# Four edits at the stage boundaries of a convolution and attention kernel: who writes a place-holding tile, when the next image's norm is computed, when the feed-forward begins, and who gathers the last image's rest

## The chip, the cores and the metric

The kernel runs on one core of a Trainium2 chip. The metric is the device time in microseconds of one execution. Times given for the whole kernel are medians of several executions; durations of single instructions come from one profiled execution. TensorE is called PE, VectorE DVE, ScalarE ACT, GpSimd POOL and SyncE SP, as in the profile.

## The reference

The input is four images of 128 channels by 64x64 points (4096 tokens), float32. Each image goes through a non-local layer whose scores compare all tokens with all tokens; the whole then goes through an attention layer with its feed-forward, and through a linear layer with a batch norm and a scan. Of the reference, shortened:

```python
# layer 0, on the group-normalised image
y = einsum('oc,nchw->nohw', w, x) + b; e1, e2, asm = prelu(y)   # w1/w2 (64 rows), wa (128 rows)
score = softmax(einsum('nci,ncj->nij', e1, e2), axis=2)
out = einsum('nij,ncj->nci', score, asm)
# attention over 1024 tokens, 16 heads of size 8, q = k = v
q = qz_ring(heads + rx_theta)              # products of cosines
attn = softmax(q q^T / sqrt(8)); ctx = attn q
x1 = ln(x + ctx @ w_comb.T + b_comb)
zf = cos(x1[..., :8]) * cos(ry_theta)
out = ln(x1 + relu(zf @ w1.T + b1) @ w2.T + b2)
# then Wx = x W, batch norm over all rows, and a scan along the rows with V
```

## The kernel before

The images are worked one after the other, in three stages each; lines are those of the kernel before.

`first_stage` (L1178) is the convolution layer of one image. The image `xs` is normalised to `q` by eight DVE instructions (L331), which need the group statistics: means `gm` and, from POOL's power function (L228), the inverse deviation `r_g`. Then eight pieces give `e1` and `e2`: a matmul (L343), two ACT relus (L294, L295: `ya`/`za` and `yb`/`zb`), one DVE addition (L296); this is the `prelu` of L291. Four pieces give `asmT` (matmuls L351 and L360, then `prelu_vector`: DVE L300 and L301). Then 128 pieces of scoring: a score matmul pair (L384), ACT's exponential (L392), DVE's running sum (L400), and the weighing matmul (L407). After each of these 140 pieces the code calls `meanwhile()`, which issues one step of the image's own next work, and one step of the feed-forward of the image before. `in_steps(waiting, every, most)` hands these out: a new chunk of the feed-forward is begun every `every` calls, at most `most` are open, and every open chunk makes one step per call. There are eight chunks of 27 steps. Of those, DVE's heavier ones are step 2 (the addition `v` L990) and 3 (statistics of `v`), 5 (the normalisation), 7 to 10 (the cosine), 18 (an addition and statistics), 20, 22 and 24 (normalisations and statistics). Step 9 is a sine on ACT, step 17 the matmuls L1042, steps 25 to 27 transposes, the linear layer and its batch norm statistics.

`second_stage` (L1224) is the attention. It works eight pairs of heads, each in four blocks of tokens. PE computes scores (L867), ACT their exponentials (L879), PE the weighing (L720). The score matrix is symmetric: for blocks off the diagonal DVE flips the exponentials (L686) and PE weighs the flipped ones too (L699); these mirror sums are added into `later` (L713). When a block's own sums are complete, `finish` transposes them (`o`, L754) and POOL copies them in 16 pieces into `own` (L762). `mirrored` gathers what the mirror sums give for that block: POOL adds row sums (L736, L741), copies them in 16 pieces (L747), DVE transposes `later` (L777), POOL copies 16 pieces (L787) and adds them (L789, L790). `result` divides (DVE, L794 and L795). For the last pair, three blocks' `mirrored` run at the end of the stage one after the other, each into a `room` of its own, and their three `result` functions are left over: `im["left"]`. The next `first_stage` takes them at its calls 10, 14 and 18.

The next image is prepared in the last block of the last pair: `upcoming` steps through its load (`load_x`, whose issue waits on PE's release of memory) and `norm_stats` (eight statistics L307, their mean L310, and through PE two small products `pg` and `pv`, L312 and L321). `r_g` is computed behind it.

The order of PE, DVE and ACT within these two stages is written by hand (`tc.manual_schedule`): each engine issues its instructions in the order of the code. POOL is ordered by hand in the attention, and by a planner in the convolution. [...] Memory of a stage is laid over the memory of the stage before, and the first writer of a tile waits until the earlier tiles there were read. In `first_stage` one tile, `gap` (6144 floats per partition), holds no data. It stands in the layout so that the tiles behind it come to lie in space that is free early; its first column is written once (L1191), ahead of everything else of the stage.

The last image has no convolution behind it. `third_stage` (L1262) takes its three results and then its feed-forward, eight chunks begun at once, ordered by the planner on all engines. There `fx` is the loaded input of a chunk with a bias added by POOL (L980), `cT` the transposed context (ACT, L983), `v` the sum (L990), `less_v`/L265 its normalisation on ACT with `r_v` from POOL (L228). `hold_every` loads the results of the first three images for the scan (L1287, six loads issued by ACT). The scan follows.

Of the kernel before, what the change touches and what calls it, by code (L numbers as in the profile page):

```python
# [26 lines left out]
def kernel(  # L27
# [31 lines left out]
    nc = tc.nc  # L59
# [264 lines left out]
    def layer0(n, xs, xh, norm, shifted, begin, meanwhile):  # L324
# [23 lines left out]
        for i in range(NIC // 2):  # L348
            pc = pair_psum(f"pa{n}_{i}")
            for j in range(2):  # L350
                nc.tensor.matmul(  # L351
                    pc[:, j, :],
                    ones[ds(32 * j, 1), :],
                    ba_row[ds(32 * j, 1), :].unsqueeze(1).broadcast_to([1, TG, P]),
                    start=True,
                    stop=False,
                    skip_group_check=True,
                )
            for k in range(2 * TG):
                nc.tensor.matmul(  # L360
                    pc[:, k // TG, ts(k % TG, P)],
                    xh[:, ts(2 * TG * i + k, P)],
                    wa_sb,
                    start=False,
                    stop=True,
                    skip_group_check=True,
                )
            to = asmT[:, ts(i, 2 * IC)].rearrange("p (a b) -> p a b", a=2)
            prelu_vector(to, pc, mid_tile(f"za{n}_{i}"), aa_sb)
            meanwhile()  # L370

        if shifted:
# [186 lines left out]
    def attention(n, q, xs, tail, upcoming):  # L559
# [170 lines left out]

            return 2 * NT + (b - NQB // 2) * TG

        def mirrored_sums(pair, b, denom):

            total = small.tile([P, QT, 2], F32, tag="by_key", name=f"by_key{n}_{pair}_{b}")
            nc.gpsimd.tensor_tensor(  # L736
                total, denom[:, ts(b, QT), :], denom[:, ds(NT + b * QT, QT), :], ALU.add
            )
            if b >= NQB // 2:
                odd = total[:, TG:QT, :]  # L740
                nc.gpsimd.tensor_tensor(odd, odd, denom[:, ds(third_sum(b), TG), :], ALU.add)  # L741
            by_token = small.tile([P, QT, 2], F32, tag="by_token", name=f"by_token{n}_{pair}_{b}")
            src = total.rearrange("p (x s) h -> p s x h", s=4)
            dst = by_token.rearrange("p (x a) h -> p a x h", a=4)
            for a in range(4):
                for s in range(4):
                    nc.gpsimd.tensor_copy(dst[ts(s, 32), a], src[ts(a, 32), s])  # L747
            return by_token

        def finish(pair, b, block, later, denom):  # L750


            o = half_tile(f"o{n}_{pair}_{b}")
            nc.vector.transpose(o, block["acc"])  # L754

            tag = f"own{b}" if b < 2 else "own"
            own = once.tile([P, QT, 2, V], F32, tag=tag, name=f"own{n}_{pair}_{b}")
            ov = o.rearrange("p (s a m) -> p s a m", s=4, a=4)
            for h in range(2):
                for x in range(2):  # L760
                    for s in range(4):
                        nc.gpsimd.tensor_copy(  # L762
                            own[ts(s, 32), ts(x, 4), h, :], ov[ts(2 * h + x, 32), s, :, 0:V]
                        )

            def mirrored(room=None):
                while any(g["steps"] and g["block"] <= (pair, met_by[b][-1]) for g in groups):
                    run_flips(TG)
                    run_pending(turn + 2, 16)
                sums = mirrored_sums(pair, b, denom)  # L770


                if room is None:
                    turned = get("turned", f"turned{n}_{pair}_{b}")
                else:
                    turned = room[:, 0 : 2 * P]
                nc.vector.transpose(turned, later[:, ts(b, 2 * P)])  # L777
                tv = turned.rearrange("p (y k a d) -> p k y a d", y=2, k=4, a=4)
                if room is None:
                    other = get("other", f"other{n}_{pair}_{b}")  # L780
                else:
                    other = room[:, ds(2 * P, QT * 2 * D)]
                to = other.rearrange("p (y a h d) -> p h y a d", y=2, a=4, h=2)
                for x in range(2):
                    for h in range(2):
                        for k in range(4):
                            nc.gpsimd.tensor_copy(to[ts(k, 32), h], tv[ts(2 * x + h, 32), k])  # L787
                    at = other.rearrange("p (t h d) -> p t h d", h=2, d=D)
                    nc.gpsimd.tensor_tensor(own[:, :, :, 0:D], own[:, :, :, 0:D], at, ALU.add)  # L789
                nc.gpsimd.tensor_tensor(own[:, :, :, D], own[:, :, :, D], sums, ALU.add)  # L790

            def result():
                inv = small.tile([P, QT, 2], F32, tag="inv", name=f"inv{n}_{pair}_{b}")
                nc.vector.reciprocal(inv, own[:, :, :, D])  # L794
                nc.vector.tensor_tensor(  # L795
                    qb[:, ts(b, QT), ts(pair, 2 * D)].rearrange("p t (h d) -> p t h d", d=D),
                    own[:, :, :, 0:D],
                    inv.unsqueeze(3).broadcast_to([P, QT, 2, D]),
                    ALU.mult,
                )  # L800

            if b == 2:
                ends.append((turn + 8, mirrored))
                ends.append((turn + 12, result))
            elif b > 2:
                late[0:0] = [mirrored, result]
            else:
                late.extend([mirrored, result])
# [40 lines left out]
        for pair in range(NPAIR):  # L849
            keys, queries, qa, later, denom = ready  # L850
            for b in range(NQB):
# [7 lines left out]
                for at, unit in enumerate(tiles):  # L859
# [4 lines left out]
                    for h in range(2):  # L864
                        for x in range(2):
# [5 lines left out]
                                start=True,  # L871
                                stop=True,
                            )
                    es = exps(name, end_of_all and at >= 2)

                    split = off and unit[0] != unit[1]
                    for h in range(2):
# [54 lines left out]
                    if tail and turn > 2 and next(tail, tail) is tail:  # L932
                        tail = None
                        rest()
                    if end_of_all and (at == 2 or at >= QT):
                        next(upcoming, None)
                    fresh = {
                        "in": block,
# [11 lines left out]
                ready = upcoming_pair  # L950
        for it in waiting:
            weigh(it)
        finish(*it["block"])
        while flips or pending:
            next(upcoming, None)
            run_flips(TG)
            run_pending(turn + 2, 16)
        for _ in upcoming:
            pass
        for _, end in ends:  # L960
            end()
        rooms = (None, half_tile(f"room0_{n}"), get("later", f"room1_{n}"))
        for mirrored, room in zip(late[0::2], rooms):
            mirrored(room)
        return late[1::2]

    def feed_forward(im, i, t2_rows, last, final):
# [210 lines left out]
    def first_stage(im, before):  # L1178


        n = im["n"]


        ffn = dict(x1=(HALF, 2), fhalf=(HALF, 6), hT=(MID, 2))
        sums = dict(sums=(MID, 2), half=(HALF, 2), thalf=(HALF, 6))
        rest = dict(e=(BIG, 2), big=(BIG, 1), mid=(MID, 5))
        pools = {**ffn, "gap": ((P, GAP), 1), **rest, **sums}
        psum = dict(ps_acc=(ONE, 1), ps_pair=(MID, 2), ps_one=(ONE, 2), ps_tok=(ONE, 1))
        engines = {nc.tensor.engine, nc.scalar.engine, nc.vector.engine}
        with stage(f"conv{n}", **pools, **psum), tc.manual_schedule(engines=engines):  # L1190
            nc.vector.memset(get("gap", f"gap{n}")[:, 0:1], 0.0)  # L1191
            own, calls = [], [0]
            step_late = in_steps(feed_forwards(before) if before else [], 15, 2)

            def meanwhile(steps=1):

                calls[0] += 1
                if before and calls[0] in (10, 14, 18):
                    before["left"].pop(0)()
                for _ in range(steps):  # L1200
                    step_first(own)
                step_late()

            norm = im["norm"] or list(norm_stats(n, im["xs"]))[-1]
            layer0(
                n,
                im["xs"],
                im["q"],
                norm,
                n == "r",  # L1210
                lambda ic, sums: own.append(tokens(im, ic, sums)),
                meanwhile,
            )
            *own, tail = own
            for g in own:
                for _ in g:
                    pass
            while step_late():
                pass
            while not next(tail):  # L1220
                pass
        return tail
# [39 lines left out]
    def third_stage(im, final):  # L1262

        with stage(
            f"ffn{im['n']}",
            x1=(HALF, NTG),
            fhalf=(HALF, 22),
            hT=(MID, 6),
            ps_one=(ONE, 8),
        ):  # L1270
            for f in im["left"]:
                f()
            step = in_steps(feed_forwards(im, final), 1, NTG)
            while step():
                pass

# [248 lines left out]
```

## Time and profile before

| | |
|---|---|
| median of 3 executions | 7322.82 us (7321.42 to 7324.19) |
| the profiled execution, and its span | 7318.31 us, 7316.6 us |
| mean granted clock of PE | 0.98 |
| PE busy | 6989.7 us, 96% |
| DVE, ACT, POOL busy | 5984.1, 5890.0 and 2772.9 us (82, 81 and 38%) |
| scoring of image 0, first to last (no feed-forward beside it) | 61.56 to 434.8: 373.24 us, PE busy 369.5 |
| scoring of images 1, 2 and 3 (each with a feed-forward) | 469.16, 468.79 and 469.73 us, PE busy 444.3, 443.8 and 444.6 |
| third score pair of images 0 to 3 at | 61.56, 1739.84, 3535.21 and 5320.27 us |
| first `ya` (L294) of images 0 to 2 at | 31.85, 1694.25 and 3500.28 us |
| last `o` (L754) of the last image at | 7037.77 us |

A line of the timeline gives the start of an instruction or a run of equal ones, its length, the engine, the line of the code, the operation, what it writes and reads, and in brackets how long the engine had been idle before it and whose completion ended that. A line of the list of waits gives the engine, its tile and line, then the releasing engine and tile, then the total, the number of waits and the longest. A busy share says nothing of a stage by itself: windows of time have to be compared, and a stage where PE is full is bound by PE even if others are nearly full too.

### The profile page before, as it was taken

The page shows a single profiled execution, that of the slowest core. Times are in us where ns is not written, and L with a number is a line of the kernel's source. Part 1 is how long each engine was busy: PE and PEld are TensorE (multiplying, and loading weights), DVE is VectorE, ACT ScalarE, POOL GpSimd, SP SyncE. Part 2 cuts the span into 40 slices and gives each one's busy share as a digit, 9 for nine tenths or more (in the row PEclk, how much of TensorE's full clock was granted, in tenths as well). Part 3 has the DMA queues.
Part 4 walks back from the last instruction along what each step waited for, and adds up shares of the span by engine and source line. Part 5 has one row for each costly group of instructions (what it writes and reads, how often), then busy time and mean ns, then how long its engine had stood idle before and what let it go on. Part 6 is the DMA issues. An engine that isn't in the chain of part 4 may idle for free. (4 is left out here: it accounts for less than half of the span.)

```text
span 7316.6 us, 225003 instructions
## 1 busy us (share of the span) xinstructions
PE 6989.7 (96%) x93198; PEld 3500.9 (48%) x93198; DVE 5984.1 (82%) x8068; ACT 5890.0 (81%) x11605; POOL 2772.9 (38%) x9929
## 2 busy tenths in 40 slices
PE   8999999998999999999899999999899999999977
PEld 3445555554444555554344455555444455555546
DVE  5678899886778999888677998989777798889964
ACT  3479999994448999998444999999744599999966
POOL 1024444433223454444222354444422344444442
PEclk9999999999999999999999999999999999999988
DMA  1010000000111000000011100000001100000012
GB/s 28 32 35 24 29 20 21 21 20 14 35 40 44 27 21 20 21 24 20 18 32 48 37 21 21 20 27 18 18 26 35 44 32 21 24 29 21 11 59 105
DMA packets 81599, 212.82 MB, mean 29 GB/s; under 512 B 8800, under 2 KB 8832, under 8 KB 79792
## 3 DMA queue, kind: packets, MB, share of 16 engines
q1 hardware_dynamic: 77312, 186.68, 7.5%
q8 instruction: 733, 12.01, 0.7%
q10 hardware_dynamic: 2016, 10.49, 0.4%
q14 instruction: 306, 2.51, 0.1%
q0 software_dynamic: 1232, 1.14, 0.1%
HBM read 141.65 MB, written 56.62 MB: 27 GB/s over the span
## 5 line engine op out<-in xcount | busy, mean ns | idle before, releaser
L879 ACT ACTIVATE e<-s 128x1024 f32<-128x1024 f32 (+1 forms) x3480 | 2946.7, 889 | 59.1 <-PE s L867 35.9
L686 DVE STREAM_TRANSPOSE t<-e 128x1024 f32<-128x1024 f32 x2240 | 2586.3, 1207 | 6.3 <-ACT e L879 3.9
L699 PEld LDWEIGHTS misc<-t,mirror 128*32 128x32 f32 x57344 | 1665.3, 110 | 1403.7 <-issue 1348.6
L699 PE MATMUL misc<-t,mirror 128*32 128x128 f32 x57344 | 1998.7, 274 | 24.9 <-DVE later L713 17.4
L879 ACT ACTIVATE xs<-s 128x1024 f32<-128x1024 f32 (+1 forms) x2152 | 1834.9, 893 | 33.0 <-PE s L867 19.6
L686 DVE STREAM_TRANSPOSE t<-xs 128x1024 f32<-128x1024 f32 x1344 | 1558.2, 1207 | 2.2 <-ACT xs L879 0.8
L720 PE MATMUL acc<-e,q_aug 128*32 128x512 f32 x11360 | 1518.5, 606 | 0.0
L867 PE MATMUL s<-queries,keys 32*128 32x512 f32 x9216 | 1216.9, 494 | 4.1 <-ACT e L879 2.7
L762 POOL COPY own<-o 32x36 f32<-32x36 f32 x2048 | 429.7, 210 | 1750.3 <-DVE o L754 1670.3
L407 PE MATMUL acc<-p,asmT 128*128 128x512 f32 x2048 | 983.3, 612 | 0.0
L392 ACT ACTIVATE p<-s 128x1024 f32<-128x1024 f32 x512 | 497.1, 1022 | 558.5 <-PE s L384 549.6
L720 PE MATMUL acc<-xs,q_aug 128*32 128x512 f32 x7072 | 942.2, 605 | 0.0
L400 DVE TENSOR_TENSOR total<-total,p 128x1024 f32<-128x1024 f32 x448 | 575.2, 1284 | 295.2 <-ACT p L392 271.5
L867 PEld LDWEIGHTS s<-queries,keys 32*128 32x128 f32 x9216 | 479.8, 182 | 490.5 <-issue 367.3
L656 POOL COPY mirror<-q 32x128 f32<-32x128 f32 x2048 | 601.1, 293 | 239.0 <-PE misc L699 151.1
L787 POOL COPY other<-turned 32x64 f32<-32x64 f32 x1920 | 441.1, 230 | 629.4 <-DVE turned L777 550.3
L879 ACT ACTIVATION_READ_ACCUMULATOR e<-s 128x1 f32 x2880 | 649.9, 226 | 0.0
L407 PEld LDWEIGHTS acc<-p,asmT 128*128 128x128 f32 x2048 | 361.5, 192 | 517.2 <-issue 515.0
L384 PE MATMUL s<-e,e 64*128 64x512 f32 x2048 | 520.3, 626 | 5.6 <-DVE asmT L301 5.4
L713 DVE TENSOR_TENSOR later<-later,misc 128x128 f32<-128x128 f32 (+1 forms) x576 | 162.5, 282 | 378.1 <-PE misc L699 373.7
L747 POOL COPY by_token<-by_key 32x4 f32<-32x4 f32 x2048 | 374.5, 183 | 86.4
L720 PEld LDWEIGHTS acc<-e,q_aug 128*32 128x32 f32 x11360 | 225.7, 108 | 347.8 <-issue 330.2
(246 smaller groups left out, 4719.1 us busy)
## 6 DMA issues: line engine op xcount, KB each, us to landing
keys<-parts_dram SPq DMA_DIRECT2D x256, 256.0 KB
queries<-parts_dram SPq DMA_DIRECT2D x1024, 32.0 KB
fx<-x_dram SPq DMA_DIRECT2D x64, 256.0 KB
x_dram<-x SPq DMA_DIRECT2D x56, 256.0 KB
xs<-in_x_dram SPq DMA_DIRECT2D x16, 512.0 KB
t_dram<-t2T SPq DMA_DIRECT2D x32, 256.0 KB
t2s<-t_dram SPq DMA_DIRECT2D x16, 512.0 KB
parts_dram<-high SPq DMA_DIRECT2D x28, 256.0 KB
```

The lines of the kernel that those rows point to most:

```text
L384: nc.tensor.matmul(s[:, j, :], e2[rows, ts(2 * jp + j, P)], e1[rows, ts(ic, IC)], start=True, stop=True,)
L392: nc.scalar.activation(p, s, AF.Exp)
L400: nc.vector.tensor_tensor(state[ic], state[ic], p, ALU.add)
L407: nc.tensor.matmul(state["acc", ic], asmT[:, ts(2 * jp + j, P)], p[:, j, :], start=jp == 0 and j == 0, stop=jp == NP - 1 and j == 1,)
L656: nc.gpsimd.tensor_copy(wv[ts(a, 32), s, :, :, ts(a, D)], own[ts(s, 32)])
L686: nc.vector.transpose(group["e"][h][:, k, :], es[h])
L699: nc.tensor.matmul(state["acc"][ts(2 * x + h, 32), :], state["w"][:, QT * (s // 4) + TG * x + s % 4, h, :], state["e"][h][:, :, ds(IC * x ...
L720: nc.tensor.matmul(it["in"]["acc"][ts(2 * h + x, 32), :], it["qa"][:, ds((2 * it["tiles"][x] + h) * V, 32)], it["e"][h][:, ts(x, IC)], sta ...
L762: nc.gpsimd.tensor_copy(own[ts(s, 32), ts(x, 4), h, :], ov[ts(2 * h + x, 32), s, :, 0:V])
L787: nc.gpsimd.tensor_copy(to[ts(k, 32), h], tv[ts(2 * x + h, 32), k])
L867: nc.tensor.matmul(ss[h][:, x, :], keys[unit[x] // QT].bitcast(F32R)[r, ts(unit[x] % QT, P)], queries[b].bitcast(F32R)[r, :], start=True, ...
L879: nc.scalar.activation(es[h][:, ts(x, IC)] if split else es[h], ss[h][:, x, :] if split else ss[h].rearrange("p x c -> p (x c)"), AF.Exp, ...
```

## The change

Six things are edited:

- The write of the `gap` tile's first column moves from DVE's queue to POOL's.
- In `meanwhile`, the feed-forward of the image before starts at the ninth call, that is behind the eight `e1`/`e2` pieces; its chunks are begun every 14 calls, not every 15; and the left-over results are taken at calls 13, 15 and 17.
- In the attention's last block, `upcoming` is stepped at the units 0 and 6 to 13, where it was at 2 and from 8 on. At the end of the stage the remaining flips are issued, then the rest of `upcoming` (statistics and norm), and only then `finish` and the pending weighing. The exponentials of that block use the `exps` tiles throughout; this changes no instruction.
- Two of the four `asmT` pieces use `prelu` (two ACT relus and a DVE addition) in place of `prelu_vector` (two DVE instructions).
- For the last image, the three `mirrored` rounds at the end are done by three engines: the first by DVE, the second by POOL, the third with copies by ACT and additions by DVE. For the other images all three stay on POOL.
- In `third_stage` the feed-forward's first two steps are issued ahead of the left-over results, and two more steps behind each of them.

```diff
--- before.py
+++ after.py
@@ -366,7 +366,10 @@
                     skip_group_check=True,
                 )
             to = asmT[:, ts(i, 2 * IC)].rearrange("p (a b) -> p a b", a=2)
-            prelu_vector(to, pc, mid_tile(f"za{n}_{i}"), aa_sb)
+            if i % 2:
+                prelu_vector(to, pc, mid_tile(f"za{n}_{i}"), aa_sb)
+            else:
+                prelu(to, pc, mid_tile(f"ya{n}_{i}"), mid_tile(f"za{n}_{i}"), (0.0, 0.0), aa_sb)
             meanwhile()
 
         if shifted:
@@ -730,21 +733,21 @@
 
             return 2 * NT + (b - NQB // 2) * TG
 
-        def mirrored_sums(pair, b, denom):
+        def mirrored_sums(pair, b, denom, copy, tt):
 
             total = small.tile([P, QT, 2], F32, tag="by_key", name=f"by_key{n}_{pair}_{b}")
-            nc.gpsimd.tensor_tensor(
+            tt(
                 total, denom[:, ts(b, QT), :], denom[:, ds(NT + b * QT, QT), :], ALU.add
             )
             if b >= NQB // 2:
                 odd = total[:, TG:QT, :]
-                nc.gpsimd.tensor_tensor(odd, odd, denom[:, ds(third_sum(b), TG), :], ALU.add)
+                tt(odd, odd, denom[:, ds(third_sum(b), TG), :], ALU.add)
             by_token = small.tile([P, QT, 2], F32, tag="by_token", name=f"by_token{n}_{pair}_{b}")
             src = total.rearrange("p (x s) h -> p s x h", s=4)
             dst = by_token.rearrange("p (x a) h -> p a x h", a=4)
             for a in range(4):
                 for s in range(4):
-                    nc.gpsimd.tensor_copy(dst[ts(s, 32), a], src[ts(a, 32), s])
+                    copy(dst[ts(s, 32), a], src[ts(a, 32), s])
             return by_token
 
         def finish(pair, b, block, later, denom):
@@ -763,11 +766,11 @@
                             own[ts(s, 32), ts(x, 4), h, :], ov[ts(2 * h + x, 32), s, :, 0:V]
                         )
 
-            def mirrored(room=None):
+            def mirrored(room=None, copy=nc.gpsimd.tensor_copy, tt=nc.gpsimd.tensor_tensor):
                 while any(g["steps"] and g["block"] <= (pair, met_by[b][-1]) for g in groups):
                     run_flips(TG)
                     run_pending(turn + 2, 16)
-                sums = mirrored_sums(pair, b, denom)
+                sums = mirrored_sums(pair, b, denom, copy, tt)
 
 
                 if room is None:
@@ -784,10 +787,10 @@
                 for x in range(2):
                     for h in range(2):
                         for k in range(4):
-                            nc.gpsimd.tensor_copy(to[ts(k, 32), h], tv[ts(2 * x + h, 32), k])
+                            copy(to[ts(k, 32), h], tv[ts(2 * x + h, 32), k])
                     at = other.rearrange("p (t h d) -> p t h d", h=2, d=D)
-                    nc.gpsimd.tensor_tensor(own[:, :, :, 0:D], own[:, :, :, 0:D], at, ALU.add)
-                nc.gpsimd.tensor_tensor(own[:, :, :, D], own[:, :, :, D], sums, ALU.add)
+                    tt(own[:, :, :, 0:D], own[:, :, :, 0:D], at, ALU.add)
+                tt(own[:, :, :, D], own[:, :, :, D], sums, ALU.add)
 
             def result():
                 inv = small.tile([P, QT, 2], F32, tag="inv", name=f"inv{n}_{pair}_{b}")
@@ -871,7 +874,7 @@
                                 start=True,
                                 stop=True,
                             )
-                    es = exps(name, end_of_all and at >= 2)
+                    es = exps(name, end_of_all)
 
                     split = off and unit[0] != unit[1]
                     for h in range(2):
@@ -932,7 +935,7 @@
                     if tail and turn > 2 and next(tail, tail) is tail:
                         tail = None
                         rest()
-                    if end_of_all and (at == 2 or at >= QT):
+                    if end_of_all and (at == 0 or 6 <= at < 6 + NIC):
                         next(upcoming, None)
                     fresh = {
                         "in": block,
@@ -950,18 +953,23 @@
                 ready = upcoming_pair
         for it in waiting:
             weigh(it)
-        finish(*it["block"])
-        while flips or pending:
-            next(upcoming, None)
+        while flips:
             run_flips(TG)
-            run_pending(turn + 2, 16)
         for _ in upcoming:
             pass
+        finish(*it["block"])
+        while pending:
+            run_pending(turn + 2, 16)
         for _, end in ends:
             end()
         rooms = (None, half_tile(f"room0_{n}"), get("later", f"room1_{n}"))
-        for mirrored, room in zip(late[0::2], rooms):
-            mirrored(room)
+        engines = [(nc.gpsimd.tensor_copy, nc.gpsimd.tensor_tensor)] * 3
+        if n == N - 1:
+
+            engines[0] = (nc.vector.tensor_copy, nc.vector.tensor_tensor)
+            engines[2] = (nc.scalar.copy, nc.vector.tensor_tensor)
+        for mirrored, room, by in zip(late[0::2], rooms, engines):
+            mirrored(room, *by)
         return late[1::2]
 
     def feed_forward(im, i, t2_rows, last, final):
@@ -1188,18 +1196,19 @@
         psum = dict(ps_acc=(ONE, 1), ps_pair=(MID, 2), ps_one=(ONE, 2), ps_tok=(ONE, 1))
         engines = {nc.tensor.engine, nc.scalar.engine, nc.vector.engine}
         with stage(f"conv{n}", **pools, **psum), tc.manual_schedule(engines=engines):
-            nc.vector.memset(get("gap", f"gap{n}")[:, 0:1], 0.0)
+            nc.gpsimd.memset(get("gap", f"gap{n}")[:, 0:1], 0.0)
             own, calls = [], [0]
-            step_late = in_steps(feed_forwards(before) if before else [], 15, 2)
+            step_late = in_steps(feed_forwards(before) if before else [], 14, 2)
 
             def meanwhile(steps=1):
 
                 calls[0] += 1
-                if before and calls[0] in (10, 14, 18):
+                if before and calls[0] in (13, 15, 17):
                     before["left"].pop(0)()
                 for _ in range(steps):
                     step_first(own)
-                step_late()
+                if calls[0] > 8:
+                    step_late()
 
             norm = im["norm"] or list(norm_stats(n, im["xs"]))[-1]
             layer0(
@@ -1268,9 +1277,15 @@
             hT=(MID, 6),
             ps_one=(ONE, 8),
         ):
+            step = in_steps(feed_forwards(im, final), 1, NTG)
+
+            if final:
+                step()
+                step()
             for f in im["left"]:
                 f()
-            step = in_steps(feed_forwards(im, final), 1, NTG)
+                step()
+                step()
             while step():
                 pass
```

## The prediction

> **What bounds the kernel now.** I read the page's totals and slices first. TensorE (PE) is busy for 96% of the span, at a mean granted clock of 0.98. The slices hardly fall below 8 except at the end, so a lasting gain can only come from the few places where PE is empty. The windows by stage show where those are.
>
> ```profile
> 1650.00:1700.00 50.00, 37.71 (x537) 21.18 (x534) 33.99 (x53) 24.61 (x54) 28.21 (x102) 0.86 0.01 1
> 1700.00:1750.00 50.00, 36.71 (x151) 17.71 (x150) 28.98 (x45) 24.62 (x27) 16.59 (x49) 0.93 0.02 6
> 3000.00:3050.00 50.00, 50.00 (x896) 25.88 (x888) 47.51 (x55) 49.12 (x101) 34.74 (x156) 1.00 0.05 20
> 3450.00:3500.00 50.00, 17.26 (x284) 10.72 (x277) 19.81 (x35) 5.95 (x17) 32.15 (x130) 0.69 0.00 1
> 5250.00:5300.00 50.00, 28.23 (x219) 15.42 (x214) 21.96 (x47) 14.08 (x15) 33.56 (x128) 0.76 0.02 6
> 7050.00:7100.00 50.00, 11.49 (x52) 9.65 (x52) 24.41 (x79) 10.22 (x23) 41.20 (x100) 0.57 0.34 138
> ```
>
> The columns are the window, its length, then busy time and instructions of PE, its weight loads, DVE, ACT and POOL, then the clock. Inside the attention (3000) PE is full: nothing done there shows in the time. From one image's attention to the next image's convolution PE is busy for 37.7, 36.7, 17.3 and 28.2 of 50 us, and behind the last attention for 11.5; POOL is the busiest engine in three of these. What the others wait for there stands in the list of waits:
>
> ```profile
> PEld pca L343 <- DVE q L331: 48.1, 9, 28.7
> DVE gap L1191 <- POOL own L789: 33.4, 3, 23.8
> ACT ya L294 <- PE pca L343: 108.2, 7, 44.3
> DVE v L990 <- POOL own L789: 23.7, 2, 11.8
> ACT v L265 <- DVE less_v L262: 31.1, 6, 20.0
> ```
>
> (Total wait, times, longest.) The timeline between images 1 and 2 gives the chain:
>
> ```profile
> 3463.65 0.16 DVE L226 TENSOR_SCALAR v_g<-pv 128x1 f32<-128x1 f32 x1 [0.22 <-PE pv L321]
> ...
> 3493.90 0.06 DVE L1191 MEMSET gap<- 128x1 f32 x1 [23.80 <-POOL own L789]
> 3494.05 5.77 DVE L331 TENSOR_SCALAR q<-xs,gm,r_g 128x512 f32<-128x512 f32 x8
> ...
> 3496.69 3.55 PE L343 MATMUL pca<-q,w_sb 128*128 128x512 f32 x4 [28.40 <-DVE q L331]
> ...
> 3500.28 1.12 ACT L294 ACTIVATE ya<-pca,b_sb 128x1024 f32<-128x1024 f32 x1 [44.34 <-PE pca L343]
> ```
>
> A memset of one column, whose tile only keeps a place, waits 23.8 us for memory that POOL reads until then, in DVE's queue ahead of the normalisation L331. The statistics were ready at 3463.8. The waiting work is POOL's `mirrored`, about 9.3 us three times.
>
> [...] the 16 small copies L747 take 3.50 us alone and 5.35 beside L331. [...] four `pca` matmuls take 3.55 us behind the idle 28.4, and 1.88 in the next group. [...] here a 128x1 copy on DVE (L314) takes 0.16 us.
>
> **Between the images.** Three edits go together: the memset goes to POOL's queue, the norm chain (statistics, `pg`, `pv`, `r_g`) goes ahead of the last weighing and of `finish`, and the feed-forward starts at the ninth call. DVE then has L331 right behind `v_g`. For 1 to 2: the last flip ends near 3460; the chain from L310 to `v_g` takes 2.8 us (3461.01 to 3463.81), less 0.3 for an addition that stood between, so `v_g` ends near 3462.6. POOL's `r_g` (0.56) no longer stands behind the 16 copies L762 (3.96 us): 3463.2. In the trace the first `ya` comes 6.2 us behind the start of L331 (3494.05 to 3500.28). With 0.9 for L713's additions, which fall between, and 0.3 for issue, it comes at 3470.6 instead of 3500.28. From `ya` to the third score matmul pair, from where PE paces the work, image 0 without any feed-forward takes 29.7 us (31.85 to 61.56). I add 1.7 for the four feed-forward steps that remain there: 3502.0. Before, it is 3535.21. Gain **33**.
>
> For 0 to 1 the memset waited only 4.82 us (POOL works the other two blocks later, so that L331 came at 1689.83 and `ya` at 1694.25), but POOL's end (1712.2) then holds the feed-forward's first addition:
>
> ```profile
> 1712.03 0.69 DVE L990 TENSOR_TENSOR v<-pw,fx 128x512 f32<-128x512 f32 x1 [11.85 <-POOL own L789]
> ```
>
> DVE queues its pieces behind it, ACT's `zb` waits 8.84, PE 9.14. After: `v_g` 1677.0, `r_g` 1677.6, L331 from 1677.8; `ya` 4.4 behind it in the trace, plus 0.9 for L713 and 1.4 for 32 weighing matmuls on PE: 1684.5. The eight pieces then need no POOL result, so they end by 1701 (before, 1722.8). POOL still ends near 1711.6, and in the changed order the same addition waits for it, now between two `asmT` pieces: it would start about 1707 and so waits 4.7, of which I count 4.1: 1684.5 + 29.7 + 4.1 = 1718.3, where 1739.84 was. Gain **21.5**. The wait's bounds are 0 and 9 us, so the gain's are 16.5 and 25.6. 2 to 3 has the same waits (4.82, 11.85): **21.5** again. Sum 76, with bounds of about 60 and 85.
>
> What is late next is POOL: its three rounds aren't shortened, only taken off DVE's queue. Behind the moved memset POOL queues mirror copies and the memsets L585 and L590 (0.60 and 1.80 us), then `r_v`; these have the pieces as cover. Without cover, 2.4 us each. Behind the norm chain PE waits about 1.4 us more for `tv`; DVE queues `o` and with it POOL's 16 copies 1 us later. Both are inside the sum. The exponentials' changed condition and the shift of eight statistics in the last block move no work across an engine; the block is PE-full, with DVE at 47.5 of 50 only in its middle: cost 0, up to 3 each if the image's load (PE releases it; that wait is 3.0) is late for the earlier steps.
>
> **Feed-forward in 132 calls with spacing 14.** The first chunk's eight steps that left the pieces now lie in the scoring, where PE is 444.3 of 469.2 us busy: about 25 us of idle against 3.7 in image 0. 216 steps cause 25 us less 4, so 8 steps add 0.8; the sine moved there adds a pair of table loads (1.28 each by its row) on ACT, which idles: 0 to 3. Spacing 15 puts the heavy steps (statistics 1.8 with addition 0.7; 2.5; norm 1.1) of two chunks in the same call: some 4.3 us of DVE beside its 1.28 for the sum, over PE's 3.67 per call. Spacing 14 keeps them apart, a gain of 4 (0 to 12) per image, or a loss up to 5 if other pairs fall together. Net **0**, from -8 to +12 for each of three images. DVE is at 344 of 469 us, so its mean has room.
>
> **`asmT`'s prelu.** For two of four pieces L300 (1.28) and L301 (1.22) become two ACT relus (1.11 each) and one L296 (1.28). DVE saves 1.22 twice per image; PE paces `asmT` at 3.04 us per piece in image 0, so I take **0** (bounds -2 and +3 per image).
>
> **The tail.** POOL does three `mirrored` rounds, and with the `fx` additions between them ends at 7079.2; `r_v` of the first chunk, ready to be computed at about 7062, comes at 7072.40, and the first L265 at 7074.71, 20 us late. The load of the scan's input is issued at 7079.02. After, DVE does one round, POOL one, ACT the copies of the third. DVE: 32 copies at 0.16 to 0.22 (from the 128x1 and 128x256 rows) are 5 to 7 us, for which it was idle. ACT: no row shows a 32-partition copy there. [...] ACT's queue behind them holds `cT` and L265, and ACT was idle for 20. POOL: own copies to 7042.2, sums and 16 copies to 7047 (with contention), seven `fx` additions of 1.26 (8.8), 16 copies (4.2), additions (1.1): `r_v` at 7061 instead of 7072.4, an estimate 11 earlier. Behind it the chunks follow every 4.4 us, with POOL fewer additions to make; last `v` 7108.74 before, 7094 after. Gain **15**, bounds 5 and 22. Later stages (matmul groups L1042 some 6 us apart, scan, output) start earlier as a whole.
>
> **Sum.** 33 + 21.5 + 21.5 + 0 + 0 + 15 = 91 us. The profiled execution took 7318.31 (span 7316.6 and 1.7 around it); it becomes 7227. The runs' median is 4.5 above the profiled one, so 7322.8 - 91 = **7232**; its own range 7212 to 7252.
>
> **Rivals.** (A, 0.60) The forecast.
> (B, 0.14) POOL's rounds take the place of the memset: `v` L990 and `r_v` wait for all that `ya` gained, and each boundary gives some 11 less. For: two 11.85 waits, POOL ends no sooner. Against: eight pieces stand ahead. 91 - 33 = 58: **7265**.
> (C, 0.15) The spread feed-forward is worth 12 per image: PE's idle in the scoring halves. For: 15.4 us of waits of `pl` for `q` per image, behind DVE's queue. 91 + 36 = 127: **7196**.
> (D, 0.07) The tail gives nothing, because ACT's small copies hold `cT` (32 at 0.5 are 16 us): 91 - 15 = 76: **7247**.
> (E, 0.04) Slower. The feed-forward, squeezed into 132 calls, meets itself so that DVE, in order, holds `total` and so PE's next scores. For 24 chunks to eat 91 us each must cost 3.8 us more; from there it decides; at 5 us: -120, **7352**. Against: before, 24 chunks cost about 64 in all.
>
> **Numbers.** Runs of this kernel tell changes of about 0.2% (14.6 us) from none. A to D are all faster by more; between them and E little lies near zero: faster 0.94, same 0.02, slower 0.04. The range takes in C and B at their points: 7196 to 7267.
>
> **What would show it.** Right: no wait of L331 for POOL; the first `ya` near 1684.5, 3470.6, with PE 30 of 50 us busy in 3450 to 3500; third score pairs 21, 33, 21 us sooner relative to the attention's end; the scoring's lengths within 8 of 469; `r_v` of the last image's first chunk about 24 us behind the last `o`, not 34.6. Wrong: L990 waits over 9 us for POOL; the scoring grows by over 10; ACT's copies over 0.4 us each.

## The result, and the profile after

The changed kernel takes **7299.02 us** (median of 7, 7297.86 to 7299.83) where the kernel before took 7322.82: 23.8 us or 0.3% less, ratio 0.9967 with a 95% interval of 0.9957 to 0.9977. The prediction said 7232, range 7196 to 7267. The sign was right and the size was not: 91 us were forecast. The profiled execution took 7298.87 us, its span 7297.2.

The same windows of the changed kernel (window, length, busy time and instructions of PE, its weight loads, DVE, ACT and POOL, clock, DMA share and GB/s):

```profile
1650.00:1700.00 50.00, 44.39 (x558) 21.94 (x551) 39.34 (x57) 34.13 (x63) 26.67 (x80) 0.93 0.01 1
1700.00:1750.00 50.00, 39.74 (x165) 19.76 (x164) 27.20 (x45) 20.63 (x23) 22.64 (x72) 0.86 0.02 6
3450.00:3500.00 50.00, 44.20 (x456) 23.42 (x453) 37.17 (x52) 30.08 (x49) 35.77 (x104) 0.97 0.02 5
5250.00:5300.00 50.00, 38.52 (x266) 20.72 (x267) 27.32 (x44) 23.18 (x24) 37.46 (x123) 0.88 0.02 6
7050.00:7100.00 50.00, 21.78 (x92) 16.64 (x92) 37.86 (x153) 26.91 (x79) 35.08 (x45) 0.53 0.41 155
```

PE is busier in all five: 44.2 where 17.3 stood between images 1 and 2, 21.8 where 11.5 stood in the tail. The memset's wait is gone from the list of waits, and the wait of `ya` has fallen from 108.2 to 55.3:

```profile
ACT ya L294 <- PE pca L343: 55.3, 5, 14.6
...
PE s L387 <- DVE asmT L301: 21.2, 4, 9.2
...
DVE v L998 <- POOL own L792: 21.2, 2, 10.7
```

The two lines of 21.2 belong together. L998, the first addition of the feed-forward, waits for POOL for about as long as before (23.7 us in all), but now it stands between two `asmT` pieces. PE's scores wait for the piece behind it: 21.2 us, where before it was

```profile
PE s L384 <- DVE asmT L301: 5.4, 4, 1.7
```

The memset's wait is repaired, but most of the forecast gain is missing. I cut both traces into stretches, with marks that both kernels have: the attention's last weighing matmul, the image's fourth score pair (L384, now L387) and last score matmul, the attention's first score.

| stretch | before, by image | after, by image | sum of the changes |
|---|---|---|---|
| attention's end to fourth score pair | 69.8, 79.1, 70.0 | 55.8, 47.2, 56.1 | -59.8 |
| fourth to last score pair, images 1 to 3 | 468.5, 468.5, 468.7 | 485.4, 484.9, 485.0 | **+49.6** |
| attention, images 0 to 3 | 1236.2, 1239.8, 1238.6, 1239.8 | 1238.0, 1241.0, 1239.8, 1239.9 | +4.3 |
| last attention's end to the program's end | 278.9 | 264.8 | -14.1 |

With 0.5 at image 0's start they sum to -19.5, the difference of the two spans (19.4). The boundaries and the tail gain 74 us; the scoring, counted at nothing, takes 50 back.

### The profile page after: what moved, and what is told of

It is laid out like the page before. It is cut to its first block, busy times and chain, and to the rows that moved or that the text cites. A ratio compares the mean times of both kernels' runs of the same rounds, so it can differ in the third digit from the quotient of the medians.

```text
span 7297.2 us, 224976 instructions
## 1 busy us (share of the span) xinstructions
PE 7005.9 (96%) x93198; PEld 3505.6 (48%) x93198; DVE 5997.3 (82%) x8097; ACT 5906.1 (81%) x11647; POOL 2795.8 (38%) x9860
## 5 line engine op out<-in xcount | busy, mean ns | idle before, releaser
L882 ACT ACTIVATE e<-s 128x1024 f32<-128x1024 f32 (+1 forms) x3480 | 2946.7, 889 | 63.9 <-PE s L870 39.8
L882 ACT ACTIVATE xs<-s 128x1024 f32<-128x1024 f32 (+1 forms) x2152 | 1835.2, 893 | 32.8 <-PE s L870 19.6
L765 POOL COPY own<-o 32x36 f32<-32x36 f32 x2048 | 434.3, 212 | 1724.4 <-DVE o L757 1644.1
L790 POOL COPY other<-turned 32x64 f32<-32x64 f32 x1904 | 449.1, 236 | 631.3 <-DVE turned L780 552.8
L387 PE MATMUL s<-e,e 64*128 64x512 f32 x2048 | 526.6, 633 | 24.8 <-DVE asmT L301 21.2
L750 POOL COPY by_token<-by_key 32x4 f32<-32x4 f32 x2016 | 373.9, 185 | 85.0
```

The lines of the kernel that those rows point to most:

```text
L387: nc.tensor.matmul(s[:, j, :], e2[rows, ts(2 * jp + j, P)], e1[rows, ts(ic, IC)], start=True, stop=True,)
L765: nc.gpsimd.tensor_copy(own[ts(s, 32), ts(x, 4), h, :], ov[ts(2 * h + x, 32), s, :, 0:V])
L882: nc.scalar.activation(es[h][:, ts(x, IC)] if split else es[h], ss[h][:, x, :] if split else ss[h].rearrange("p x c -> p (x c)"), AF.Exp, ...
```

## The experiments

Theory 1 is that the feed-forward's new layout lengthens the scoring; theory 2 blames other edits (the prelu on ACT, or the new calls of the left-over results). Theory 1 has four forms: the spacing of 14 (1a); the later start, because steps move to where PE is full (1b), or with a fixed cost for every call of delay (1c); or how the feed-forward's steps fall on the steps of the image's own tokens, which recur every 16 calls (1d).

### The feed-forward's layout

`after_ff_as_before`, the whole layout put back:

```diff
-step_late = in_steps(..., 14, 2)
+step_late = in_steps(..., 15, 2)
-if before and calls[0] in (13, 15, 17):
+if before and calls[0] in (10, 14, 18):
-if calls[0] > 8:
-    step_late()
+step_late()
```

> The changed kernel with the feed-forward laid out as it was: from the first call, every 15 calls, left-over results at 10, 14, 18. In the changed kernel each scoring with a feed-forward takes some 16.5 us more than before (from its fourth score pair to its last: 485 against 468.5). Theory 1 (the new layout of the feed-forward costs that): scoring back to 468 to 470. The first chunk's addition L998 then comes at the second call and waits for POOL, which costs the boundaries 10 to 20 us each, so the total is about 7290 to 7310. Theory 2 (the prelu on ACT or the results' new calls cost it): scoring stays at 485 and the total is 7330 or more.

Measured: 7297.71 (7297.0 to 7299.41). Scoring 468.6, 468.1 and 468.6; boundaries 68.2, 71.1 and 68.2. Theory 1 holds: the layout costs the 50 us, and at the boundaries it gives 48. The two cancel within 2 us, so this edit, on which most of the boundaries' gain rests, moves no time in the end.

`after_spacing15` (`14` to `15` alone) and `after_begun_first_call` (the condition `calls[0] > 8` removed alone) part the two:

> The changed kernel with a chunk begun every 15 calls instead of 14, still from the ninth call. Theory 1a (the spacing of 14 is what costs: chunks meet each other and the image's own steps, of period 16, in a worse way): scoring back to 470 to 475, total 7299 - 45 = 7254, less a few us for the last chunk, which now ends one call past the scoring. Theory 1b (the later start is what costs: eight steps of the first chunk and all chunks pushed into the phase where PE is full): scoring stays at about 485, total 7299.

> The changed kernel with the feed-forward from the first call, every 14 calls. Theory 1a (spacing): scoring stays near 480 to 485, the boundaries lose 10 to 20 us each to the wait for POOL: 7330 to 7350. Theory 1b (late start): scoring back to about 470, total 7285 to 7305.

Measured: 7315.6 and 7293.29. With spacing 15 scoring stays at 484.1, 482.2 and 484.2, and the last chunk's end adds 5 to 8 us behind it. With a start at the first call it is 466.5, 465.6 and 466.1. So the start makes it, not the spacing (1a is out), and not the results' new calls, which this kernel keeps. With a start at the first call spacing 14 is worth about 2 us per image (466.1 against 468.4). With a start at the ninth its scoring is 1.6 longer than with 15, and 6.4 less stand behind it. The window from the fourth to the last score pair of image 1 shows of what the 19 us consist; first with a start at the first call, then as changed:

```profile
1742.84:2209.36 466.52, 444.05 (x1701) 202.63 (x1698) 349.72 (x748) 215.39 (x249) 134.02 (x135) 0.98 0.12 38
```

```profile
1729.02:2214.41 485.39, 451.33 (x1709) 205.77 (x1706) 351.83 (x756) 216.92 (x252) 140.58 (x143) 0.97 0.11 34
```

PE is busy for 7.3 us more, and idle for 34.1 us instead of 22.5. Of the 7.3, four `pz` and four `ph` matmuls that lay ahead of the scoring are 2.7; the score matmuls, equal in number, take 1.8 more. DVE is only busy for 2.1 more: it isn't its mean that decides.

### Amount or meeting?

Four starts more, each by one number in `if calls[0] > 8:` (4, 12, 16, 15).

> The changed kernel with the feed-forward begun at the fifth call instead of the ninth. From the fourth score pair to the last, scoring takes 466 us with a start at the first call and 485 at the ninth (both every 14 calls). Theory 1c (density: each call of delay costs 19/8 = 2.4 us): 475. Theory 1d (phase: each step moved into the scoring costs about 0.5 us, and the rest of the 19 is how the chunks' steps fall on the steps of the image's own token work, which have a period of 16 calls): no monotonic course, anything from 468 to 490. The boundaries are as with a start at the first call, since the first addition again waits ahead of pieces: 68 to 74 from the attention's end to the fourth pair. Total 7340 by density.

> The feed-forward begun at the thirteenth call, behind the four asmT pieces too. Boundaries: no piece stands behind the wait for POOL any more, 46 us instead of 56, 47 and 56. Scoring by density (1c): 495, total about 7310; by phase (1d): 466 + 12 steps of 0.5 = 472 if the phase is a good one, total about 7240, and up to 500 if it is a bad one.

> The feed-forward begun at the seventeenth call: shifted by a whole period of 16 against a start at the first call, so that its steps meet the same steps of the token work. By phase (1d): scoring 466 + 16 steps of 0.5 = 474, and some us for the last chunk's end behind the last piece; boundaries 46: total about 7250. By density (1c): 466 + 16 x 2.4 = 504, total about 7340.

> The changed kernel with the feed-forward begun at the sixteenth call. Starts at calls 1, 5, 9, 13 and 17 gave a scoring of 466, 472, 485, 483 and 473 us, with 8.5 us more behind the last piece for 17. By phase (1d) a start at 16 is one call off the good phase of 1 and 17 and ends within the 140 calls: scoring 473 to 478, nothing behind it, boundaries 45: total 7250 to 7266. If the course is not one of phase: above 480, 7275 or more.

Measured (scoring is the mean of three images; "behind" is how much longer than its usual 8.0 us it takes from the last score to the attention's first):

| start at call | scoring | behind | boundaries | total |
|---|---|---|---|---|
| 1 | 466.1 | 0 | 68.9, 73.7, 68.2 | 7293.29 |
| 5 | 472.4 | 0 | 63.9, 65.4, 65.8 | 7295.92 |
| 9 (the change) | 485.1 | 0 | 55.8, 47.2, 56.1 | 7299.02 |
| 13 | 482.9 | 0 | 49.1, 48.6, 47.1 | 7278.98 |
| 16 | 479.5 | 5 | 46.6, 44.7, 44.7 | 7277.84 |
| 17 | 472.6 | 8.5 | 44.9, 45.9, 46.2 | 7265.92 |

A fixed cost for every call (1c) is out: it foresaw 495 for a start at 13 and 504 at 17. The scoring alone rises and falls again, but with what stands behind it the starts from 9 to 17 give 485, 483, 485 and 481. From the thirteenth call on all steps of the feed-forward lie behind the pieces, so an amount that is full there (1b) could give this too. These starts alone don't decide between 1b and 1d. A start at 16 was expected inside 473 to 478 with nothing behind; both were missed. From the thirteenth call on no piece waits for POOL, as expected: of L998's wait for it 4.9 us are left at 13, behind all the pieces, and none at 16 and 17.

`after_begun_call17_sp13` (start 17, spacing 13):

> The feed-forward begun at the seventeenth call, every 13 calls, so that the last chunk ends seven calls earlier. The end behind the last piece (8.5 us) goes. By phase, each chunk now moves three calls against the period of 16 instead of two, so that other steps meet: fewer chunks in a row in a bad place, but more in all; scoring 470 to 485, total 7255 to 7275. By density alone it would not change: 473, total 7257.

Measured: 7412.05, slower than before. This was an error in my layout, and it decides nothing between the theories. A chunk has 27 steps and two may be open; at spacing 13 the third is due in the call in which the first makes its 27th step, is refused, and is next asked for 13 calls later. Scoring falls to 451 and 74 us of feed-forward stand behind it, where nothing covers them. With 27 steps and two open chunks, 14 is the tightest spacing that works.

What meets can be read in the trace. This is DVE of the changed kernel in two successive calls of image 1's scoring, which take 13.9 us here, and below it what PE waits for:

```profile
1952.13 1.75 DVE L237 SCALAR_TENSOR_TENSOR r<-k,r 128x512 f32<-128x512 f32 x1
...
1954.53 0.18 DVE L1013 TENSOR_TENSOR z<-v,be_bc 128x32 f32<-128x32 f32 x1
...
1956.56 0.68 DVE L1071 TENSOR_TENSOR t<-q,fx 128x512 f32<-128x512 f32 x1
...
1959.08 2.55 DVE L403 TENSOR_TENSOR total<-total,p 128x1024 f32<-128x1024 f32 x2
...
1961.95 1.56 DVE L542 TENSOR_TENSOR q<-q,r 128x64 f32<-128x64 f32 x3
1963.44 1.61 DVE L255 TENSOR_SCALAR q<-t,mv_w,r_w 128x128 f32<-128x128 f32 x4
```

```profile
1957.79 1.88 PE L410 MATMUL acc<-p,asmT 128*128 128x512 f32 x4
1964.06 1.52 PE L273 MATMUL pl<-ident,q 128*128 128x128 f32 x4 [4.39 <-DVE q L255]
...
1966.55 2.68 PE L387 MATMUL s<-e,e 64*128 64x512 f32 x6
```

Three streams come together: the image's tokens (the cosine L237, the products L542), one chunk's cosine (`z` L1013 and what follows) and another chunk's `t` with its statistics and normalisation (L1071, L255). DVE has no gap over these 13 us, and PE's transposes `pl` of that chunk stand ahead of the next scores, so PE waits. Chunks come every 14 calls and token steps every 16, so each chunk moves by two calls against them, and bad meetings should form a run. I list, from the starts and ends in the traces, the calls (counted from 1, two taken together) in which PE is idle for over 2 us:

```
start 1:  39 (3.1) 55 (2.1) 93 (2.3) 109 (5.1)
start 9:  13 (10.1, the wait of L998) 45 (2.3) 61 (6.2) 75 (5.2) 89 (5.1) 103 (3.2) 119 (2.1) 133 (3.0)
start 17: 41 (5.1) 55 (3.1) 71 (2.1) 109 (2.3) 125 (5.1)
```

With a start at the ninth call the whole run (2.3, 6.2, 5.2, 5.1, 3.2, 2.1) lies in the scoring. With a start at 1 or 17, as I read it, part of it falls on the calls before 30, where no token step runs yet, or past the feed-forward's end.

To test that, the token steps were shifted instead of the feed-forward:

```diff
 def tokens(im, i, sums):
     ...
+    for _ in range(8 if i == 0 and n in (1, 2, 3) else 0):
+        yield
     yield
```

`after_tokens_8_later` has this on the changed kernel, `after_call1_tokens_8_later` with the start at the first call, and `after_call13_tokens_12_later` has 12 and a start at the thirteenth.

> The changed kernel with the images' own token steps eight calls later (images 1 to 3), the feed-forward still from the ninth call. By phase the two then meet as with a start at the first call: scoring 466 + 8 steps of 0.4 = 469 to 472 instead of 485, total about 7299 - 42 = 7257. If where the feed-forward's work lies decides: scoring 485, total 7299.

> The other way: the feed-forward from the first call, where scoring took 466 us, and the token steps eight calls later. By phase they then meet as in the changed kernel: scoring about 480, total 7293 + 42 = 7335. If the place of the feed-forward's work decides: 466, total 7293.

> The feed-forward from the thirteenth call, so that no piece waits for POOL (boundaries 49, 49, 47), and the token steps twelve calls later. By phase: scoring 466 + 12 steps of 0.4 = 471 to 474 instead of 483; total 7279 - 30 = about 7249, the best so far. If place decides: 7279.

Measured: 7263.8, 7302.4 and 7248.84. With the feed-forward left where it was, the scoring falls from 485.1 to 474.1, 472.0 and 473.8, and PE's idle time in image 1's scoring from 34.1 to 24.4. DVE again runs 756 instructions in that window, and PE 1708 where it ran 1709; only POOL has 26 fewer. With as much work on DVE and PE, the meetings are 12 of the 19 us. The list above, made for this kernel, has 15.4 us in the scoring, where a start at the ninth call alone has 27.1. For the other 7, the later start by its amount (1b) stays open. The reverse test agrees only in sign: 472.5, 468.1 and 470.1 where I expected 480. A bare phase modulo 16 is thus too simple; presumably it counts how much of the run lies where all three streams are at work, but I have no formula for it that gives both numbers. The third kernel is the fastest, 1.0% under the kernel before (ratio 0.9901, 0.9884 to 0.9917): scoring 469.5, 466.1 and 468.2, some 2 us more behind it, boundaries near 48.5.

### The other edits

`before_gap_pool`: the kernel before, with `nc.vector.memset` of the gap tile as `nc.gpsimd.memset`.

> The kernel before with one edit: the one-column memset of the gap tile on POOL. If the memset's waits (33.4 us in sum) were worth their length, 7322.8 - 33 = 7290. If the feed-forward's first addition L990, which stands at the second call, takes the wait over (POOL's rounds end no sooner, and later where DVE now works beside them), the gain is 0 to 10 us: 7313 to 7323, with L990 waiting over 60 us for POOL in all.

Measured: 7314.63, 7.8 us less (the kernel before took 7322.44 in the same series). The wait that took the memset's place stands in its list of waits (before: 23.7, 2, 11.8):

```profile
DVE v L990 <- POOL own L789: 40.7, 2, 20.3
```

It wasn't over 60 in all, but a single one reached 20.3. Between images 1 and 2 `ya` comes 25.6 us sooner, but from the attention's end to the fourth score pair the three boundaries take 74.1, 73.4 and 70.4 us where they took 69.8, 79.1 and 70.0: 1 us gained in sum, because the addition L990 stands ahead of the pieces. The two profiled executions differ by 2.9 us, and I can't place the rest of the 7.8.

`after_norm_late` (the attention's end and `upcoming` as before) and `after_asm_vector` (`prelu_vector` for all four pieces):

> The changed kernel with the norm's chain as before: upcoming stepped at 2 and from 8, finish and its 16 copies on POOL ahead of r_g. Then L331 waits for r_g behind the copies: 4 to 5 us at each of three boundaries, while the attentions take back the 1.2 to 1.8 us by which they have grown: total 7299 + 8 to 11 = 7307 to 7310. If the norm's place is worth nothing because the pieces wait for POOL in any case: 7295 to 7300.

> The changed kernel with all four asmT pieces by the two DVE instructions, as before. The prediction counted this edit at 0, from -2 to +3 per image: 7297 to 7308. If the ACT relus are what makes the pieces or the scoring longer: 7290 or less.

Measured: 7299.09 and 7297.42. The kernel before took 7319.2 in this series and 7322.8 in the first, so both edits are worth nothing within about 4 us. Between images 1 and 2 of `after_norm_late` L331 comes 2 us later, and yet `ya` 0.7 sooner, while in the changed kernel 128 weighing matmuls stand between its first two `pca` matmuls and the next; the attentions shrink by 3.1 in sum. I had put 8 to 11 us on the norm's place: a miss.

`after_tail_pool` (the two `engines[...]` lines taken out):

> The changed kernel with all three of the last image's rounds on POOL, as before. From the last attention's end to the program's end the changed kernel takes 264.8 us, the kernel before 278.9. If the three engines are worth the 14 us: 279 and a total of 7313. If the feed-forward's steps issued ahead of the results are worth part of it: in between, 7303 to 7310.

Measured: 7310.07, the tail 275.1. The three engines are worth 10 to 11 of the 14 us. The rest, 3.8, may be the steps issued ahead of the results; that wasn't tried alone.

## Why the prediction was wrong

**The boundaries**, forecast 33, 21.5 and 21.5, gave 31.9, 14.0 and 13.8 at the fourth score pair (32.8, 15.0 and 14.7 at the third, where the prediction counted). Between images 1 and 2 the chain was right: the first `ya` came at 3475.84, which is 3469.5 once the 6.3 us are taken off by which the attention ended later; 3470.6 was forecast. At the other two the failing step is "POOL still ends near 1711.6 ... and so waits 4.7". POOL ended at 1721.12, and the addition waited 10.45, past the bound of 9:

```profile
1678.70 5.55 POOL L765 COPY own<-o 32x36 f32<-32x36 f32 x16
...
1688.43 3.97 POOL L790 COPY other<-turned 32x64 f32<-32x64 f32 x8
...
1698.85 6.49 POOL L750 COPY by_token<-by_key 32x4 f32<-32x4 f32 x16
...
1720.89 0.23 POOL L793 TENSOR_TENSOR own<-own,by_token 128x16 f32<-128x16 f32 x1
```

```profile
1720.97 0.69 DVE L998 TENSOR_TENSOR v<-pw,fx 128x512 f32<-128x512 f32 x1 [10.45 <-POOL own L792]
```

The same runs before:

```profile
1675.16 4.00 POOL L762 COPY own<-o 32x36 f32<-32x36 f32 x16 [8.89 <-DVE o L754]
...
1684.27 2.11 POOL L787 COPY other<-turned 32x64 f32<-32x64 f32 x8 [0.44 <-DVE turned L777]
...
1690.04 5.35 POOL L747 COPY by_token<-by_key 32x4 f32<-32x4 f32 x16
...
1711.96 0.23 POOL L790 TENSOR_TENSOR own<-own,by_token 128x16 f32<-128x16 f32 x1
```

POOL's end came 8.9 us later than before. Of these, 2.3 are the attention's own later end, 1.3 the later start of the copies behind the norm chain, and 5.4 POOL's work: from the first copy to the last addition 42.4 us, where it took 37.0. The runs took 5.55, 3.97 and 6.49 us for 4.00, 2.11 and 5.35 (the last kind takes 3.50 where nothing holds it up, so at 1684.89 here). They now lie beside DVE's L331 and L296, which were moved there: beside L331 seven copies L765 take 0.41 to 0.44 us each, where those behind it take 0.21. The prediction had such runs at 3.50 alone and 5.35 beside L331, and then held POOL's end fixed. The copies beside L296 are shown one by one in the last section; by what the engines hold each other up isn't shown. That the wait made the shortfall is borne out by the start at the thirteenth call, where no piece waits: the two boundaries take 49.1 and 47.1, which is 20.7 and 22.8 less than before.

A misreading adds 0.9 us to each of the three forecasts: 61.56, given for image 0's third score pair, is its second. The third begins at 62.49, so that the 29.7 us from `ya` to there are 30.6.

**The feed-forward**, forecast 0 from -8 to +12 per image, cost 16.5. The step that failed is "216 steps cause 25 us less 4, so 8 steps add 0.8": starting eight calls later cost 18.9 us in image 1, measured at spacing 14. The step has two errors. It counted PE's idle time alone, but PE was also busy for 7.3 us more, of which 2.7 are moved matmuls. And it spread the idle time evenly over the steps, while in the trace it lies in a few meetings, and grew by 11.6. I looked only for meetings of two chunks and left out the token steps of the image itself, the third stream, whose period makes the start matter. The value for the spacing (a gain of 4, from 0 to 12) was of the right size: 2 with a start at the first call, and some 5 with a start at the ninth, where all of it comes from behind the scoring. So its reason, heavy steps kept apart, is not shown there. Rival E had the right mechanism, at 2.1 us per chunk instead of the 3.8 from which it would have decided; I gave it 0.04 and an outcome past zero, with nothing between it and the forecast.

**The tail**, forecast 15, gave 14.1. `r_v` of the first chunk came 27.5 us behind the last `o` (34.6 before, about 24 forecast). ACT's 32 copies took 7.5 us, 0.19 us each for the 16 of L750 and 0.24 for the 16 of L790; what the forecast held for them was the author's estimate. DVE's took 10.7 instead of 5 to 7, because five of them ran beside POOL's additions (last section). Undisturbed, 16 copies L750 took 2.85 us and eight L790 1.59, so that 32 would be 6.0, inside the estimate. So the total was right, but DVE's term was too low; what made up for it was not separated.

**The attention**, forecast 0 with up to 3 each, took 4.3 in all; **the prelu** 0, as forecast. Rival B (POOL's rounds take the memset's place) describes `before_gap_pool`. In the changed kernel it named the right wait, but two boundaries fell some 7 us short and the third 1, not 11 each.

## What to carry to other kernels

When work is delayed so that it no longer stalls an idle stage, cost it again where it lands: its own work on the full engine, and which of its steps meet which steps of every other periodic stream there. Here streams with periods of 14 and 16 calls met in a run; moving first one stream and then the other showed what a mean can't. And when a wait is removed from one engine, reprice the other engine's work beside what now runs.

## What the runs showed of the hardware

The slowing goes both ways. In the tail DVE does two equal runs of eight 32x64 copies: the first beside POOL's five additions, the second while POOL is idle.

```profile
7041.79 6.24 DVE L790 COPY other<-turned 32x64 f32<-32x64 f32 x8
...
7049.19 1.59 DVE L790 COPY other<-turned 32x64 f32<-32x64 f32 x8
```

```profile
7041.25 6.14 POOL L988 TENSOR_TENSOR fx<-fx,bc_bc 128x512 f32<-128x512 f32 x5
7051.86 2.12 POOL L790 COPY room<-room 32x64 f32<-32x64 f32 x8 [4.47 <-DVE by_key L739]
```

The runs take 6.24 and 1.59 us, but it isn't an even slowing. In the first run four copies, each beside one addition, take 1.20 to 1.21 us and end 0.05 behind it, and the last three, behind the additions, take 0.18 to 0.19. One such pair, and the reverse between images 0 and 1, where a copy of POOL begins during a DVE instruction:

```profile
7043.69 1.26 POOL L988 TENSOR_TENSOR fx<-fx,bc_bc 128x512 f32<-128x512 f32 x1
7043.80 1.21 DVE L790 COPY other<-turned 32x64 f32<-32x64 f32 x1
```

```profile
1688.75 1.29 DVE L296 SCALAR_TENSOR_TENSOR e<-za,a_sb,ya 128x1024 f32<-128x1024 f32 x1 [1.44 <-ACT za L295]
1688.97 1.16 POOL L790 COPY other<-turned 32x64 f32<-32x64 f32 x1
...
1707.97 1.28 DVE L300 TENSOR_SCALAR za<-pa,aa_sb 128x1024 f32<-128x1024 f32 x1 [0.20 <-PE pa L360]
1708.17 0.23 POOL L790 COPY room<-room 32x64 f32<-32x64 f32 x1
```

Between 1688 and 1708 eight copies of POOL run into an L296. They take 1.08 to 1.26 us, where their neighbours take 0.18 to 0.23, and end 0.04 to 0.10 behind it. Three that begin within 0.05 us of an L296's start keep 0.18 to 0.23. Beside L300, which takes as long (1.28) but reads a matmul's result `pa` in place of `za` and `ya`, a copy keeps its 0.23. So each copy that was held up in these stretches, on DVE or on POOL, had begun second, 0.07 us or more behind the other, and lasted until the other's end. The other lost at most 0.07 us: the five additions of POOL take 1.26 to 1.27 us, as one does while DVE is idle (1.27 at 7058.08), and the eight L296 1.28 to 1.35. A copy of 0.18 us thus took up to 1.26 here, about as long as the L296 that it ran into.
